# Products of the unit matrix in TensorE's planned gaps, and a new record of moves

## The chip, the cores and the metric

The kernel runs on one core of one Trainium2 chip. The metric is the device time of one execution in microseconds (us); the time before is the median of three runs. A core has a matrix engine (TensorE, PE in the profile; its weight loads are listed apart as PEld), a vector engine (DVE), a scalar engine for functions (ACT), a general engine (GpSimd, POOL), and SyncE (SP), which issues transfers here. Each engine works through its own instructions in order, and semaphores hold an instruction back until what it needs is there.

## The reference, cut to what matters

The input is four images of 128 channels and 64 x 64 pixels (4096 tokens of 128 values each). Layer 0 is a hybrid of convolution and state-space scans, layer 1 attention with a mixture of experts. What the changed code computes is layer 0, above all this scan, one for the "seed" branch and two in a cascade for each image:

```python
z = zxbcdt[..., :di]
dt = softplus(zxbcdt[..., -nh:] + dt_bias)
xBC = silu(causal_conv3(xBC) + conv_b)          # three taps along the tokens
y = ssd(xs * dt[..., None], dt * A, Bm, Cm)     # chunks of 64 tokens, a state carried from chunk to chunk
y = y + D[None, None, :, None] * xs
y = y.reshape(b, l, di) * silu(z)
y = y * rsqrt(mean(y * y, -1) + 1e-05) * rms_w  # the mean over each token's di values
return y @ out_w.T
```

After both cascades of an image come a layer norm over channels, the addition of the seed branch, and a feed-forward part: two 1x1 convolutions with a depthwise 3x3 convolution and a GELU between them. Layer 1 follows (layer norm, four-headed attention over 4096 tokens, then eight experts with the best two chosen); no line of it is in the change.

## The kernel before, in words

Layer 0 works in blocks of 512 tokens, eight to an image, always with all 128 channels on the partitions. A block's passage through one scan is an item. Items of the seed branch come first (8 of them, for all four images at once), then the two cascades of each image, the second two blocks behind the first: 8 + 64 = 72 items. Each item passes through four stages, `outer` (loading, norm), `prep` (time steps, decays), `front` (the five products, transposes, states) and `back` (products within chunks, gate, norm, output). In one step of the loop, item s is in `front`, s - 1 in `back`, s + 1 in `prep`, s + 2 in `outer`, and the feed-forward part of the image before may run along. So one step holds one `back`; below it is called a stage of the program, and its length is that from one `ps_ms` to the next.

In `back`, lines 622 to 721, TensorE forms the products `bank` (named `py` in the code) within chunks, DVE adds their halves to `y` (`scalar_tensor_tensor` in `within`), POOL multiplies by the gate (`zs`, `nc.gpsimd.tensor_mul`), ACT squares the result into `y`, and TensorE takes the mean of the squares with the product `ps_ms`. ACT forms the reciprocal root of it, and TensorE's product `ps_out` gives the item's output. The products `ps_yo`, `ps_d`, `ps_z`, `ps_x`, `ps_B`, `ps_C`, `pt_b`, `pt_x`, `ps_g` and `ps_st` belong to `front` and to the next `back`.

The instructions are not issued as the stages call them. The class `Deck` (line 773) records every operation of layer 0 with what it depends on and with a price; a run of TensorE calls into one tile counts as one operation, `Op` (line 757). `Deck.flush` (line 911) then plays the five engines through in a small model: each takes, of its operations that are ready, the one of the highest rank, if its tiles have room in their ring of buffers. The rank is the order of recording, less an entry of the table `BEHIND` (line 878) for stage, engine and, where one is given, tile: a positive entry lets an operation wait behind later ones, a negative one draws it forward. These entries, found by a search over the model, are what the change calls the record of moves. The resulting order, `order`, is what is issued, all from one line, the call of `getattr` in `flush` (line 1040): so all of layer 0 stands under L1040 in the profile, and has to be told apart by tiles.

For TensorE the model keeps a list `worked` of busy stretches. An operation is priced at twice its cost where the last `COLD[0]` = 4.0 us held more than `COLD[1]` = 2.0 us of idle time:

```python
busy_for = sum(b - max(a, start - span) for a, b in worked)
slow = 2 if span - busy_for > most else 1
```

There are two flushes: one for the whole of layer 0 but the last image's feed-forward part, and one for that part, which runs together with the first projections of layer 1. Most short-lived products in PSUM (`ps_ms`, `ps_out`, `ps_cd`, `pt_x`, `ps_mean` and others) share one ring of two tiles, `psw`.

Of the kernel before, what the change touches and what calls it, by code (L numbers as in the profile page):

```python
# [46 lines left out]
class Spec:  # L47


    def __init__(self, nh, n, nl, row0, rows):  # L50
        self.nh, self.n, self.nl = nh, n, nl
        self.row0, self.rows = row0, rows
        self.ng = nl // 4
        self.np = nl // 2
        self.di = nh * 8

        self.iB, self.iC, self.ix, self.iz, self.idt = 0, 384, 768, 1344, 1536
        self.nw = 1536 + 128 * self.np
# [697 lines left out]

class Op:
    __slots__ = ("engine", "calls", "cost", "deps", "users", "waits", "ready", "rank", "uses", "set",
                 "phase", "stage", "mode", "out", "src", "both")

    def __init__(self, engine):
        self.engine, self.calls, self.cost, self.deps, self.users = engine, [], 0.0, set(), []
        self.ready, self.rank, self.uses, self.set, self.phase = 0.0, 0.0, {}, None, None
        self.out = self.src = self.mode = None
        self.both = False


SILU, GELU, EXPS = "silu", "gelu", "exps"
# [4 lines left out]
class Deck:  # L773


    def __init__(self, nc):
        self.nc, self.ops, self.seen, self.rings, self.ring_of = nc, [], {}, {}, {}
        self.phase, self.stage, self.held = None, None, set()
        self.make, self.made, self.both, self.count = {}, {}, {}, 0
        for name in ("vector", "scalar", "gpsimd", "tensor", "sync"):  # L780
            setattr(self, name, Recorder(self, name))

# [58 lines left out]
    def price(self, engine, name, args, kw, out, ins, op):  # L841
# [36 lines left out]
        ("back", "gpsimd"): 70, ("back", "gpsimd", "last0_casc1"): 120, ("back", "scalar"): -50,  # L878
        ("back", "scalar", "A_casc1"): -200, ("back", "scalar", "e"): -40, ("back", "sync"): 40,
        ("back", "sync", "gfd"): -10, ("back", "sync", "hl"): 120, ("back", "sync", "raw"): -40,  # L880
        ("back", "sync", "td"): 110, ("back", "tensor", "ps_d"): -70, ("back", "tensor", "ps_out"): 120,
        ("back", "tensor", "py"): 120, ("back", "vector", "A_casc1"): -200, ("back", "vector", "bdt_casc1"): 140,
        ("back", "vector", "biasB_casc1"): 40, ("back", "vector", "biasC_casc1"): 200, ("back", "vector", "raw"): 10,
        ("back", "vector", "wc_casc1"): -120, ("ffn", "gpsimd", "h1_1"): 70, ("ffn", "scalar"): 10,
        ("ffn", "sync", "gf8"): 30, ("ffn", "tensor", "ps_gmix"): 10, ("ffn", "tensor", "ps_mean"): 40,
        ("ffn", "tensor", "ps_var"): 10, ("ffn", "vector", "acc"): 140, ("ffn", "vector", "t"): -40,
        ("front", "gpsimd", "last_casc1"): -10, ("front", "scalar"): 20, ("front", "scalar", "Bc"): -20,
        ("front", "scalar", "Cc"): -400, ("front", "scalar", "bT"): -40, ("front", "scalar", "cd"): 240,
        ("front", "scalar", "rt"): -10, ("front", "scalar", "zs"): -70, ("front", "tensor"): 20,
        ("front", "tensor", "ps_ea"): -120, ("front", "tensor", "ps_g"): -120, ("front", "tensor", "ps_st"): 180,  # L890
        ("front", "tensor", "ps_x"): 20, ("front", "tensor", "ps_z"): -10, ("front", "tensor", "pt_x"): 40,
        ("front", "vector", "gm"): 20, ("front", "vector", "ps_st"): -20, ("front", "vector", "xd"): -200,
        ("front", "vector", "xp0"): -10, ("front", "vector", "xp3"): 30, ("front", "vector", "y"): -200,
        ("outer", "gpsimd"): -200, ("outer", "gpsimd", "halo_seed"): 200, ("outer", "gpsimd", "last0_casc0"): 120,
        ("outer", "scalar"): 40, ("outer", "scalar", "hi"): -120, ("outer", "scalar", "ln_r"): -20,
        ("outer", "scalar", "xin"): 200, ("outer", "sync", "raw"): 20, ("outer", "sync", "wc_seed"): -10,
        ("outer", "sync", "xin"): -40, ("outer", "tensor"): 110, ("outer", "tensor", "ps_tok"): 40,
        ("outer", "vector"): -20, ("outer", "vector", "A_seed"): 200, ("outer", "vector", "W_casc0"): 200,
        ("outer", "vector", "bdt_casc0"): 10, ("outer", "vector", "bdt_seed"): 10,
        ("outer", "vector", "biasB_casc0"): 20, ("outer", "vector", "biasB_seed"): -10,  # L900
        ("outer", "vector", "biasx_seed"): 200, ("outer", "vector", "raw"): 70, ("outer", "vector", "wc_casc0"): 10,
        ("prep", "gpsimd"): 190, ("prep", "gpsimd", "cdx"): 10, ("prep", "gpsimd", "halo_seed"): 10,
        ("prep", "gpsimd", "x4"): -40, ("prep", "scalar", "ah"): -40, ("prep", "scalar", "cde"): -70,
        ("prep", "sync", "x4"): 90, ("prep", "tensor", "ps_cd"): 10, ("prep", "vector", "acs"): -190,
        ("prep", "vector", "sdT"): -70,
    }
    LAG = 0.05
    COLD = 4.0, 2.0
# [2 lines left out]
    def flush(self, tc):  # L911
# [4 lines left out]
        opening = set()  # L916
# [11 lines left out]
        for i, op in enumerate(ops):  # L928
            op.rank = -i - self.BEHIND.get((op.stage, op.engine), 0) - self.BEHIND.get(
                (op.stage, op.engine, op.out.rsplit("_", 1)[0]), 0)  # L930
        room, head = dict(self.rings), {}
        phases, whole = {}, {}
        for op in ops:
            if op.set == SILU:
# [9 lines left out]
        now, table, lock, mode, worked = 0.0, None, None, None, deque()  # L944
        lockers = {"vector": 0.0, "gpsimd": 0.0}
        while events:
            now = events[0][0]
            while events and events[0][0] <= now + 1e-9:
                _, kind, i = heappop(events)
                op = ops[i]  # L950
                if kind == 0:
                    heappush(ready[op.engine], (-op.rank, i))
                elif kind == 1:
                    for t in op.uses:
                        left[t] -= 1
                        if left[t] == 0:
                            room[self.ring_of[t]] += 1
                    for j in op.users:
                        ops[j].waits -= 1
                        if ops[j].waits == 0:  # L960
                            lag = 0.02 if ops[j].engine == op.engine and op.engine != "sync" else self.LAG
                            heappush(events, (now + lag, 0, j))
            for e in engines:
# [3 lines left out]
                while ready[e]:  # L967
                    key = heappop(ready[e])
                    op = ops[key[1]]
# [27 lines left out]
                    continue  # L997
                i = chosen[1]
                op = ops[i]
                for t in [t for t in op.uses if t not in opening]:  # L1000
                    opening.add(t)
                    room[self.ring_of[t]] -= 1
                    head[self.ring_of[t]] = head.get(self.ring_of[t], 0) + 1
                start = now
                if e == "tensor" and op.mode != mode:
                    mode = op.mode
                    start += 0.1
                if e == "tensor":

                    span, most = self.COLD  # L1010
                    while worked and worked[0][1] < start - span:
                        worked.popleft()
                    busy_for = sum(b - max(a, start - span) for a, b in worked)
                    slow = 2 if span - busy_for > most else 1
# [19 lines left out]
        for i in order:  # L1034
            op = ops[i]
            if op.set == EXPS and table != EXPS:
                self.nc.scalar.preload_act_table_set(LNEXP)
            table = op.set or table
            for name, args, kw in op.calls:
                getattr(getattr(self.nc, op.engine), name)(  # L1040
                    *[self.real(a) for a in args], **{k: self.real(a) for k, a in kw.items()})
# [112 lines left out]
def layer0(tc, T, td, const, ident, eps, where, batches, qkv):  # L1154
# [9 lines left out]
    with ExitStack() as ctx:  # L1164
# [10 lines left out]
        both, first = const, where["const"]["ms_seed"][0]  # L1175
# [34 lines left out]
        nc.vector.tensor_add(bias2, P("n2b"), P("detok_b"))  # L1210

        deck = Deck(nc)
        nc = sh.nc = deck

        def ring(stack, name, bufs, **kw):
            return deck.ring(stack.enter_context(tc.tile_pool(name=name, bufs=bufs, **kw)), bufs, kw.get("space"))
# [303 lines left out]
        last = ring(ctx, "last", 2)  # L1520
# [525 lines left out]
```

## Time and profile before

| | |
|---|---|
| median of three runs | 8313.97 us (8304.8 to 8316.73) |
| the profiled execution | 8310.76 us, its span 8309.0 us |
| start and group norm, 0 to 200 us | TensorE busy 107.19 us, clock 0.81 |
| 200 to 476.5 us, mostly the seed items | TensorE busy 226.94 of 276.5 us, clock 0.85 |
| cascades without feed-forward, 476.5 to 1328.7 us | TensorE busy 729.94 of 852.2 us, clock 0.91 |
| cascades with feed-forward, 1328.7 to 3431.2 us | TensorE busy 1846.73 of 2102.5 us, clock 0.93 |
| the last image's feed-forward, 3500 to 3675 us | TensorE busy 153.59 of 175 us, clock 0.93 |
| layer 1, 3675 to 8309 us | TensorE busy 4489.99 of 4634 us, clock 0.99 |

The page of the profile gives an engine's busy time and its share of the span, then the span in 40 slices with a busy digit per engine (9 is 90% or more) and, as PEclk, the clock that TensorE was granted, in tenths of full speed. Rows of stretches name a start and an end, and for each engine the busy time and the number of instructions in it, the mean clock, the share of the transfer engines and GB/s. Rows in order of time give start, duration, engine, line, operation, the tile written and those read, and in square brackets the idle time of the engine before it with what ended it. A row of waits names the engine and tile that waited, what it waited for, the total in us, the number of waits, and the longest. In the profile a float32 product counts as two products with two weight loads, a transpose as one.

### The profile page before, as it was taken

What the parts mean: (1) busy time and instruction counts of PE and PEld (TensorE: products, weight loads), DVE (VectorE), ACT (ScalarE), POOL (GpSimd) and SP (SyncE); (2) the same over time, 40 slices, a digit from 0 to 9 for tenths busy, and PEclk for the clock granted to TensorE, in tenths of its full rate; (3) what the DMA queues carried; (4) which work ended last, traced back from release to release, by engine and by line L of the source; (5) the groups of instructions that cost most, each with busy time, mean ns of one, the idle gap of its engine ahead of it and who ended that gap; (6) DMA issues with size and microseconds to landing.
All of it is one profiled execution on the core that took longest, in us unless ns stands there. A gap on an engine that the chain in (4) does not pass through costs nothing.

```text
span 8309.0 us, 191474 instructions
## 1 busy us (share of the span) xinstructions
PE 7600.4 (91%) x80284; PEld 4516.6 (54%) x80284; DVE 6299.9 (76%) x11211; ACT 5103.8 (61%) x6517; POOL 4892.5 (59%) x3441
## 2 busy tenths in 40 slices
PE   5888888888888898779999999999999999999998
PEld 3566666666666666434555555555555545555554
DVE  5676768887888788776777777777777777777775
ACT  5767767777777777545555555555555555555554
POOL 1111111211122112119999999999999999999997
PEclk7889999999999899889999999999999999999999
DMA  4221112221112121145544445444545454444442
GB/s 139 83 56 48 43 53 57 54 57 54 52 55 59 54 62 46 54 133 139 129 126 124 127 123 130 127 126 126 129 121 136 122 135 122 120 116 121 116 121 59
DMA packets 306606, 800.55 MB, mean 96 GB/s; under 512 B 43985, under 2 KB 61009, under 8 KB 288849
## 3 DMA queue, kind: packets, MB, share of 16 engines
q1 hardware_dynamic: 304848, 780.94, 35.8%
q8 instruction: 633, 10.37, 0.5%
q10 hardware_dynamic: 432, 5.12, 0.2%
q14 instruction: 229, 1.87, 0.1%
q0 software_dynamic: 464, 2.25, 0.1%
HBM read 595.19 MB, written 192.94 MB: 95 GB/s over the span
## 4 chain that ended last, share of the span: by engine, by line
PE 29%; POOL 22%; issue 3%; DVE 2%; ACT 1%; DMA 1%; SPq 0%; POOLq 0%; DVEq 0%
POOL s L1894 13%; PE ps_mx L1850 7%; PE acc L1909 6%; POOL es L1896 6%; PE ps_s L1888 6%; PE ps_s L1882 3%; PE ps_e L1798 2%; PE ps_den L1922 1%; DVE mx L1852 1%; PE ps_taps L1040 1%; PE ps_sh L1869 0%; POOL parts L1712 0%; POOL cx L1714 0%; PE ps_f L1787 0%; PE ps_f L1786 0%
## 5 line engine op out<-in xcount | busy, mean ns | idle before, releaser
L1852 DVE TENSOR_REDUCE mx<-ps_mx 128x1 f32<-128x512 f32 x4096 | 2789.8, 689 | 815.0 <-PE ps_mx L1850 807.8
L1892 ACT ACTIVATE e<-ps_s 128x1024 f32<-128x1024 f32 x2048 | 1985.3, 1022 | 1715.6 <-PE ps_s L1888 1610.8
L1894 POOL TENSOR_TENSOR s<-e 128x1024 f32<-128x1024 f32 x1024 | 2442.2, 2385 | 206.7 <-ACT e L1892 203.5
L1850 PE MATMUL ps_mx<-k,q 128*128 128x512 f32 x4096 | 1876.1, 467 | 63.5 <-DVE mx L1852 25.3
L1896 POOL TENSOR_TENSOR es<-s 128x512 f32<-128x512 f32 x1024 | 1311.7, 1281 | 80.3
L1888 PE MATMUL ps_s<-q,k 128*128 128x512 f32 x4096 | 1279.5, 394 | 0.0
L1909 PE MATMUL acc<-e,V 128*32 128x512 f32 x8192 | 1095.2, 607 | 0.0
L1850 PEld LDWEIGHTS ps_mx<-k,q 128*128 128x128 f32 x4096 | 772.7, 189 | 532.1 <-DVE mx L1852 221.9
L1040 POOL TENSOR_TENSOR zs<-y,zs 128x256 f32<-128x256 f32 (+1 forms) x288 | 302.7, 1052 | 1153.0 <-DVE y L1040 1152.2
L1888 PEld LDWEIGHTS ps_s<-q,k 128*128 128x128 f32 x4096 | 772.6, 189 | 137.8 <-issue 2.9
L1040 DVE SCALAR_TENSOR_TENSOR e<-e,gm 128x1024 f32<-128x1024 f32 (+1 forms) x576 | 668.0, 1175 | 54.8 <-ACT e L1040 53.3
L1882 PEld LDWEIGHTS ps_s<-mr,ones 32*128 32x128 f32 x4096 | 201.4, 182 | 890.5 <-ACT e L1892 411.1
L1040 ACT ACTIVATE e<-ps_d 128x1024 f32<-128x1024 f32 (+1 forms) x576 | 546.5, 975 | 86.1 <-PE ps_d L1040 63.4
L1882 PE MATMUL ps_s<-mr,ones 32*128 32x512 f32 x4096 | 531.9, 496 | 20.3 <-ACT e L1892 20.3
L1040 DVE SCALAR_TENSOR_TENSOR y<-bank,const,y 128x128 f32<-128x128 f32 (+1 forms) x1152 | 364.2, 338 | 234.4 <-PE bank L1040 233.7
L1040 PE MATMUL bank<-e,xp 64*32 64x128 f32 x17408 | 459.0, 283 | 63.6 <-DVE y L1040 51.1
L1040 PEld LDWEIGHTS bank<-e,xp 64*32 64x32 f32 x17408 | 369.4, 110 | 134.9 <-DVE y L1040 73.7
L1040 PE MATMUL ps_d<-rt,lt 32*128 32x256 f32 x4352 | 406.7, 312 | 32.3 <-ACT e L1040 10.8
L1040 PEld LDWEIGHTS ps_d<-rt,lt 32*128 32x128 f32 x4352 | 294.6, 190 | 194.0 <-issue 50.1
L1909 PEld LDWEIGHTS acc<-e,V 128*32 128x32 f32 x8192 | 161.7, 108 | 362.6 <-issue 356.5
L1805 DVE SCALAR_TENSOR_TENSOR acc<-ps_e,w,acc 128x128 f32<-128x128 f32 x896 | 312.5, 349 | 47.7 <-PE ps_e L1798 15.0
L1040 DVE SCALAR_TENSOR_TENSOR acc<-h,pb,acc 128x512 f32<-128x512 f32 x448 | 330.4, 757 | 7.5
(349 smaller groups left out, 11503.7 us busy)
## 6 DMA issues: line engine op xcount, KB each, us to landing
k<-kd SPq DMA_DIRECT2D x512, 512.0 KB
x<-hl SPq DMA_DIRECT2D x256, 256.0 KB
V<-vd SPq DMA_DIRECT2D x128, 512.0 KB
cd<-raw SPq DMA_DIRECT2D x256, 256.0 KB
parts<-cd SPq DMA_DIRECT2D x128, 512.0 KB
xin<-in_x SPq DMA_DIRECT2D x128, 256.0 KB
q<-qd SPq DMA_DIRECT2D x512, 64.0 KB
hl<-hi SPq DMA_DIRECT2D x72, 256.0 KB
```

The source lines that it names most:

```text
L1040: getattr(getattr(self.nc, op.engine), name)(*[self.real(a) for a in args], **{k: self.real(a) for k, a in kw.items()})
L1798: nc.tensor.matmul(pe, lhsT=xl[:, tok], rhs=ew[:, e:e + 2, :].rearrange("p e c -> p (e c)"), start=True, stop=True)
L1805: nc.vector.scalar_tensor_tensor(acc, pe[:, 128 * j:128 * j + 128], we, acc, ALU.mult, ALU.add)
L1850: nc.tensor.matmul(p, lhsT=q4s[u][:, 128 * qt:128 * qt + 128], rhs=k4s[u][:, blk(kb)], start=True, stop=True)
L1852: nc.vector.tensor_reduce(mxs[u][:, qt, kb:kb + 1], p, AX.X, ALU.max)
L1882: nc.tensor.matmul(pts[j // 2][:, j % 2, :], lhsT=ones2[rows, :], rhs=mrows[u][rows, :], start=True, stop=False)
L1888: nc.tensor.matmul(pts[j // 2][:, j % 2, :], lhsT=k4s[u][:, 128 * kt:128 * kt + 128], rhs=q4s[u], start=False, stop=True)
L1892: nc.scalar.activation(e[:, 2 * j:2 * j + 2], pts[j], AF.Exp)
L1894: nc.gpsimd.tensor_add(s2, e[:, 0:2], e[:, 2:4])
L1896: nc.gpsimd.tensor_add(s, s2[:, 0], s2[:, 1])
L1909: nc.tensor.matmul(accs[u][32 * j:32 * j + 32, :], lhsT=Vs[u][:, 4 * g + j, :], rhs=e[:, j, :], start=g == 0, stop=g == 7)
L1922: nc.tensor.matmul(p[32 * j:32 * j + 32, :], lhsT=ones, rhs=s, start=True, stop=True)
```

## The change

Where the model sees TensorE idle before an operation that opens its output tile, the plan now puts plain products of the 128 x 128 unit matrix `ident` with itself into that tile, 128 columns wide. The operation then overwrites the tile as before (its first product has `start=True`), so nothing of what is computed changes. Their number is 60% of the gap at a price of 0.22 us, for gaps over 1 us; the gap is counted from the end of TensorE's last work or from the time when a buffer of the ring came free (`freed`), whichever is later. The model also counts them as work when it looks for slow stretches. Second, many entries of `BEHIND` are new. The same fills come into both flushes.

```diff
 class Op:
     __slots__ = ("engine", "calls", "cost", "deps", "users", "waits", "ready", "rank", "uses", "set",
-                 "phase", "stage", "mode", "out", "src", "both")
+                 "phase", "stage", "mode", "out", "src", "both", "fill")
...
-        ("back", "sync", "td"): 110, ("back", "tensor", "ps_d"): -70, ("back", "tensor", "ps_out"): 120,
-        ("back", "tensor", "py"): 120, ("back", "vector", "A_casc1"): -200, ("back", "vector", "bdt_casc1"): 140,
+        ("back", "sync", "td"): 110, ("back", "tensor", "ps_d"): -70, ("back", "tensor", "ps_out"): -70,
+        ("back", "tensor", "py"): 120, ("back", "vector", "A_casc1"): -400, ("back", "vector", "bdt_casc1"): 140,
...
+        ("back", "vector", "wc_casc1"): -120, ("back", "vector", "ys"): -130, ("ffn", "gpsimd", "h1_1"): 70,
+        ("ffn", "scalar"): 30, ("ffn", "scalar", "h1_0"): -10, ("ffn", "sync", "gf8"): 30,
+        ("ffn", "tensor", "ps_det"): -40, ("ffn", "tensor", "ps_gmix"): 10, ("ffn", "tensor", "ps_hh"): -40,
+        ("ffn", "tensor", "ps_mean"): 40, ("ffn", "tensor", "ps_var"): 20, ("ffn", "vector", "acc"): 130,
...
-        ("outer", "scalar"): 40, ("outer", "scalar", "hi"): -120, ("outer", "scalar", "ln_r"): -20,
+        ("outer", "tensor", "ps_tok"): -280, ("outer", "vector"): -20, ("outer", "vector", "A_seed"): 200,
...
-        ("prep", "gpsimd"): 190, ("prep", "gpsimd", "cdx"): 10, ("prep", "gpsimd", "halo_seed"): 10,
-        ("prep", "gpsimd", "x4"): -40, ("prep", "scalar", "ah"): -40, ("prep", "scalar", "cde"): -70,
-        ("prep", "sync", "x4"): 90, ("prep", "tensor", "ps_cd"): 10, ("prep", "vector", "acs"): -190,
-        ("prep", "vector", "sdT"): -70,
+        ("prep", "scalar", "ah"): 240, ("prep", "scalar", "cde"): -70, ("prep", "sync", "x4"): 100,
+        ("prep", "tensor", "ps_cd"): 10, ("prep", "vector", "a2"): 200, ("prep", "vector", "acs"): -190,
+        ("prep", "vector", "sdT"): -110,
...
                         if left[t] == 0:
                             room[self.ring_of[t]] += 1
+                            freed[self.ring_of[t]] = now
...
-                for t in [t for t in op.uses if t not in opening]:
+                opens_now = [t for t in op.uses if t not in opening]
+                for t in opens_now:
...
                     span, most = self.COLD
+                    op.fill = 0
+                    if self.ident is not None and op.out in opens_now:
+                        last = worked[-1][1] if worked else 0.0
+                        gap = now - max(last, freed.get(self.ring_of[op.out], 0.0))
+                        op.fill = int(0.6 * gap / 0.22) if gap > 1.0 else 0
+                        worked.append((now - 0.22 * op.fill, now))
...
+            if op.fill:
+                self.real(op.calls[0][2].get("out", op.calls[0][1][0] if op.calls[0][1] else None))
+                at = self.made[op.out]
+                at = at[:, 0, 0:128] if len(at.shape) == 3 else at[:, 0:128]
+                for _ in range(op.fill):
+                    self.nc.tensor.matmul(at, lhsT=self.ident, rhs=self.ident, start=True, stop=True)
...
         deck = Deck(nc)
+        deck.ident = ident
```

More of the change, by code (lines that the diff above doesn't have):

```diff
@@ L764, in __init__ @@
         self.out = self.src = self.mode = None
-        self.both = False
+        self.both, self.fill = False, 0
 SILU, GELU, EXPS = "silu", "gelu", "exps"
@@ L779, in __init__ @@
         self.make, self.made, self.both, self.count = {}, {}, {}, 0
+        self.ident = None
         for name in ("vector", "scalar", "gpsimd", "tensor", "sync"):
@@ L880 @@
         ("back", "sync", "gfd"): -10, ("back", "sync", "hl"): 120, ("back", "sync", "raw"): -40,
-        ("back", "sync", "td"): 110, ("back", "tensor", "ps_d"): -70, ("back", "tensor", "ps_out"): 120,
-        ("back", "tensor", "py"): 120, ("back", "vector", "A_casc1"): -200, ("back", "vector", "bdt_casc1"): 140,
-        ("back", "vector", "biasB_casc1"): 40, ("back", "vector", "biasC_casc1"): 200, ("back", "vector", "raw"): 10,
-        ("back", "vector", "wc_casc1"): -120, ("ffn", "gpsimd", "h1_1"): 70, ("ffn", "scalar"): 10,
@@ L885 @@
[L885 to L894, printed above, removed]
@@ L895 @@
-        ("outer", "scalar"): 40, ("outer", "scalar", "hi"): -120, ("outer", "scalar", "ln_r"): -20,
[L896 to L899, printed above, removed]
@@ L900 @@
-        ("outer", "vector", "biasB_casc0"): 20, ("outer", "vector", "biasB_seed"): -10,
-        ("outer", "vector", "biasx_seed"): 200, ("outer", "vector", "raw"): 70, ("outer", "vector", "wc_casc0"): 10,
-        ("prep", "gpsimd"): 190, ("prep", "gpsimd", "cdx"): 10, ("prep", "gpsimd", "halo_seed"): 10,
-        ("prep", "gpsimd", "x4"): -40, ("prep", "scalar", "ah"): -40, ("prep", "scalar", "cde"): -70,
-        ("prep", "sync", "x4"): 90, ("prep", "tensor", "ps_cd"): 10, ("prep", "vector", "acs"): -190,
@@ L905 @@
-        ("prep", "vector", "sdT"): -70,
+        ("back", "sync", "td"): 110, ("back", "tensor", "ps_d"): -70, ("back", "tensor", "ps_out"): -70,
+        ("back", "tensor", "py"): 120, ("back", "vector", "A_casc1"): -400, ("back", "vector", "bdt_casc1"): 140,
+        ("back", "vector", "biasB_casc1"): 40, ("back", "vector", "biasC_casc1"): 400, ("back", "vector", "raw"): 20,
+        ("back", "vector", "wc_casc1"): -120, ("back", "vector", "ys"): -130, ("ffn", "gpsimd", "h1_1"): 70,
+        ("ffn", "scalar"): 30, ("ffn", "scalar", "h1_0"): -10, ("ffn", "sync", "gf8"): 30,
@@ new lines @@
+        ("ffn", "tensor", "ps_det"): -40, ("ffn", "tensor", "ps_gmix"): 10, ("ffn", "tensor", "ps_hh"): -40,
+        ("ffn", "tensor", "ps_mean"): 40, ("ffn", "tensor", "ps_var"): 20, ("ffn", "vector", "acc"): 130,
+        ("ffn", "vector", "gmix"): -20, ("ffn", "vector", "t"): -40, ("front", "gpsimd"): 20,
+        ("front", "gpsimd", "last_casc1"): -10, ("front", "scalar", "Bc"): 20, ("front", "scalar", "Cc"): -400,
+        ("front", "scalar", "bT"): -40, ("front", "scalar", "cd"): 260, ("front", "scalar", "rt"): -10,
@@ new lines @@
+        ("front", "scalar", "zs"): -70, ("front", "tensor"): 20, ("front", "tensor", "ps_ea"): -120,
+        ("front", "tensor", "ps_g"): -120, ("front", "tensor", "ps_st"): 180, ("front", "tensor", "ps_x"): 20,
+        ("front", "tensor", "ps_z"): -10, ("front", "tensor", "pt_x"): 40, ("front", "vector", "gm"): 20,
+        ("front", "vector", "ps_st"): -20, ("front", "vector", "xd"): -200, ("front", "vector", "xp0"): -20,
+        ("front", "vector", "xp3"): 30, ("front", "vector", "y"): -200, ("outer", "gpsimd", "halo_casc0"): -40,
@@ new lines @@
+        ("outer", "gpsimd", "halo_seed"): 200, ("outer", "gpsimd", "last0_casc0"): 120, ("outer", "scalar"): 40,
+        ("outer", "scalar", "ln_r"): -20, ("outer", "scalar", "xin"): 200, ("outer", "sync", "raw"): 20,
+        ("outer", "sync", "wc_seed"): -10, ("outer", "sync", "xin"): -40, ("outer", "tensor"): 110,
+        ("outer", "tensor", "ps_tok"): -280, ("outer", "vector"): -20, ("outer", "vector", "A_seed"): 200,
+        ("outer", "vector", "W_casc0"): 200, ("outer", "vector", "bdt_casc0"): 10,
@@ new lines @@
+        ("outer", "vector", "bdt_seed"): 10, ("outer", "vector", "biasB_casc0"): 20,
+        ("outer", "vector", "biasB_seed"): -10, ("outer", "vector", "biasC_seed"): -10,
+        ("outer", "vector", "biasx_seed"): 400, ("outer", "vector", "wc_casc0"): 10, ("prep", "gpsimd"): 190,
+        ("prep", "gpsimd", "cdx"): 10, ("prep", "gpsimd", "halo_seed"): 10, ("prep", "gpsimd", "x4"): -40,
+        ("prep", "scalar", "ah"): 240, ("prep", "scalar", "cde"): -70, ("prep", "sync", "x4"): 100,
+        ("prep", "tensor", "ps_cd"): 10, ("prep", "vector", "a2"): 200, ("prep", "vector", "acs"): -190,
@@ L930, in flush @@
                 (op.stage, op.engine, op.out.rsplit("_", 1)[0]), 0)
-        room, head = dict(self.rings), {}
+        room, head, freed = dict(self.rings), {}, {}
         phases, whole = {}, {}
```

## The prediction

> **What bounds the kernel now.** I read first the page's busy shares and its 40 slices, to see where the changed code runs and what TensorE's clock does there:
>
> ```profile
> PE 7600.4 (91%) x80284; PEld 4516.6 (54%) x80284; DVE 6299.9 (76%) x11211; ACT 5103.8 (61%) x6517; POOL 4892.5 (59%) x3441
> ...
> PE   5888888888888898779999999999999999999998
> ...
> PEclk7889999999999899889999999999999999999999
> ```
>
> A slice is 8309.0/40 = 208 us. The changed code makes layer 0, slices 1 to 17. From slice 18 on, layer 1 isn't touched: its 4634 us stay, and so does all but a few us of the first 200. Next I asked for busy time and clock by stretches; columns are PE, PEld, DVE, ACT and POOL busy, clock, DMA share, GB/s:
>
> ```profile
> 200.00:3470.00 3270.00, 2831.20 (x52906) 2029.28 (x52904) 2537.55 (x4304) 2416.76 (x3245) 581.99 (x718) 0.92 0.19 54
> 714.80:763.40 48.60, 42.02 (x794) 30.75 (x794) 30.78 (x52) 33.75 (x43) 6.67 (x9) 0.89 0.04 13
> 902.00:947.70 45.70, 39.10 (x794) 28.50 (x794) 30.79 (x52) 33.62 (x43) 6.69 (x9) 0.95 0.04 14
> ```
>
> The main part of layer 0 has TensorE busy 2831 of 3270 us, 87%, more than any other engine (DVE 78%). The last two rows are two stages of the same kind: the same 794 products and 52, 43 and 9 operations of the other engines, with the same busy times there. TensorE alone differs: 42.02 against 39.10 us, +2.92, at clock 0.89 against 0.95; the stage is 48.60 against 45.70 long, +2.90. So time that TensorE loses to its clock is paid in full.
>
> How does the clock fall? Rows of the same view, cut where it changes:
>
> ```profile
> 2004.78:2008.19 3.41, 1.98 (x128) 1.87 (x128) 3.41 (x9) 0.61 (x3) 0.48 (x1) 1.00 0.02 5
> 2008.19:2011.61 3.42, 1.46 (x6) 0.50 (x6) 3.42 (x7) 1.85 (x4) 1.70 (x3) 1.00 0.00 0
> 2011.61:2015.02 3.41, 3.09 (x49) 1.40 (x52) 3.41 (x7) 1.49 (x3) 1.72 (x1) 0.50 0.41 154
> 2015.02:2018.43 3.41, 3.31 (x116) 2.85 (x108) 2.12 (x5) 1.79 (x3) 0.34 (x1) 1.00 0.84 259
> ```
>
> The clock is 1.00 or 0.50 and changes only on a grid of 3.41 us. A window in which TensorE worked 1.46 of 3.42 us is followed by one at half clock; that one, busy 3.09 us, by full clock again. Counting all windows from 200 to 3450 us in this way: of 118 at full clock with TensorE busy about 2.0 us or less, 79 were followed by half clock; of 682 that were busier, 3. A window therefore tolerates about 1.4 us of idle time. Between 200 and 3470 us 84 stretches at half clock begin, 522 us together (the mean clock says the same: (1 - 0.92) x 2 x 3270 = 523), and TensorE is busy in 456 of them. At full clock that work takes half: at most 228 us to win.
>
> Who makes the idle time? The waits of TensorE in 200 to 3470, then the order of time at one of them:
>
> ```profile
> PE ps_ms L1040 <- ACT y L1040: 137.4, 57, 8.8
> PE bank L1040 <- DVE y L1040: 50.8, 57, 1.4
> PE ps_st L1040 <- DVE gm L1040: 22.8, 18, 2.5
> ```
>
> ```profile
> 2004.69 2.07 PE L1040 MATMUL ps_st<-xd,bT 64*64 64x32 f32 x128 [1.11 <-DVE gm L1040]
> ...
> 2008.71 0.72 POOL L1040 TENSOR_TENSOR zs<-y,zs 128x256 f32<-128x256 f32 x1
> ...
> 2009.47 0.63 ACT L1040 ACTIVATE y<-zs 128x512 f32<-128x512 f32 x1
> 2010.15 1.08 PE L1040 MATMUL ps_ms<-y,const 128*64 128x512 f32 x4 [3.39 <-ACT y L1040]
> ```
>
> Once a stage, ps_ms waits for the square of zs, behind POOL and DVE: a fixed latency in which TensorE, in order, has nothing. Such a gap ends in the window just shown.
>
> [...]
>
> **The change part by part.** First, the fills. The changed program has 504 added products of the 128x128 unit matrix in 71 places; in its order of instructions they stand directly ahead of the first product of ps_ms nearly everywhere (4 each in 25 places, 11 each in 12). Each is two loads and two products of 128 columns. The nearest row is layer 1's product with the same matrix:
>
> ```profile
> L1787 PE MATMUL ps_f<-ident,acc x256: 274/326/378, 4003.6 to 8305.4; 128*128 128x128 f32 x128
> ```
>
> Two of these in a row take 0.49 us, so they start 0.49 - 0.326 = 0.16 us apart: 0.33 us for a fill, alone. In a row they may be denser: two 512-column products of ps_var took 1.02 us at 0.59 us each, 0.43 apart, so 128 columns 0.11 apart and a fill 0.215 us. Bounds 0.215 and 0.33 us at full clock; I take 0.215, since fills follow each other. A fill needs only the freed PSUM slot, so no new wait arises; behind it in TensorE's order stands ps_ms, which waits anyway. All fills are 108 us, hidden by those gaps so long as they are as long as planned; uncovered, they would be 108 us on the path.
>
> I set the fills ahead of each ps_ms beside the gap that the trace of before has there (69 stages from 200 us on):
>
> - A: 15 gaps over 2.5 us with 7 or more fills. Gaps 56.5 us, 172 fills = 37.0 us, leaving 1.3 us each. Half clock after them: TensorE busy 81.4 us.
> - B: 15 gaps over 2.5 us with 4 fills. Gaps 50.2, fills 12.9, leaving 2.5 each. Busy at half clock 75.0.
> - C: 15 gaps of 1.3 to 2.5 us. Gaps 28.5, 71 fills = 15.3, leaving 0.9 each. Busy 58.3.
> - D: 12 gaps under 1.3 us with 77 fills = 16.6 us in 9.9 us of gap. Busy 46.2.
> - 12 stages get none.
>
> Other idle time is (3270 - 2831 - 137)/3270 = 9%, 0.3 us of a window, so about 1.1 us may be left of a gap. C's 0.9 is below it, A's 1.3 just above and spoils a window only where it lies whole in it (2.1 of 3.41 of the phases); B's 2.5 can't be split into two parts under 1.1, only shorten what follows. I choose as averted shares 0.6 for A, 0.15 for B, 0.65 for C, 0.25 for D. Half of the busy time is won: 24.4 + 5.6 + 18.9 + 5.8 = 54.7 us. The fills longer than their gaps cost 8.1 us in D and 1.6 in C. Sum: -45 us. The 61 fills ahead of ps_tok, ps_dt and ps_ea at the start stand in waits (ps_tok 5.8 us on ACT, ps_dt 13.2 us on a DMA) and the last 39 after the last stage, among waits for transfers: I take 0 for both, bounds -6 and +3.
>
> Second, the record. New BEHIND entries move operations. In the stages that I compared, TensorE's order is the same but for single operations (ps_dt, ps_hh, ps_mean, pt_sd); ScalarE swaps lt, u and ah just ahead of the square y, DVE moves acc, ys, a and sd, some a third of its rows; 59 SyncE rows move past others, in transfers that use 0.19 of the DMA engines here. Nothing in the trace prices it: an operation in the chain to y moved by one place is about 0.7 us a stage (sd and u are 0.71 and 0.72), 50 us over 72 stages, with either sign; I take 0, with bounds of 25 us, since the moves ahead of y differ among stage kinds.
>
> The profiled execution took 8310.76 us (span 8309.0 plus 1.8 around it); 8310.76 - 45 = 8266, and the median of the three runs is 3 us above it: 8269 us.
>
> **Rivals.** More: at 0.33 us a fill, A's gaps close (0.95), B's leave 2.0 (0.45), C 0.9: 38.7 + 16.9 + 26.2 + 7 = 89, less overruns of about 22: -67, 8247 us. For it: gaps repeat exactly at 3.39 and 3.7 us; against it: D.
>
> Nothing: the moves lengthen the chain to y by 0.6 us a stage, 43 us, and take the gain: 8310 us. For it: DVE is 100% busy in the window before the wait; against it: TensorE's order hardly moved.
>
> Slower: the fills themselves become the path. TensorE is in order; a fill that stands where the real gap is short holds up ps_ms, ps_out and the next stage's ps_d. D is this already. If the changed order brings y earlier than planned in most stages, 80 us of the 108 lie on the path and some 55 are won: 8339 us. It decides when over half of the fills overrun their gaps.
>
> **How the numbers follow.** The likeliest, 0.55: 8269, own range 8250 to 8292. More, 0.15. Nothing within 0.2% (17 us, about what a measurement of this kernel can tell from no change), 0.15. Slower, 0.15. Hence faster 0.70, same 0.15, slower 0.15. The range 8215 to 8328 takes in "more" with a kind bound of the moves, and most of "nothing".
>
> **What would show it.** In 200 to about 3430 us: clock 0.95 instead of 0.92; TensorE's wait of ps_ms for y shrinks by about 75 us, with fills in its place; half-clock stretches fall from 84 to about 55; fills start at 0.22 to 0.33 us; stage lengths of the 714.8 kind become those of 902.0. I am wrong if the clock rises and the stages don't shorten (then another engine bounds), if fills stand where y was already there, or if layer 1 changes.

## The result, and the profile after

The changed kernel takes 8240.58 us, the median of four runs (8232.76 to 8252.73); before, the four runs shown with it have a median of 8309.38 (8302.88 to 8316.73). The ratio is 0.9924, with a 95% interval of 0.9906 to 0.9941: faster by 0.76%, about 63 us by the ratio and 69 us by the medians. Forecast were 45 us.

The busy shares and slices of the page after the change:

```profile
PE 7645.5 (93%) x81292; PEld 4619.0 (56%) x81292; DVE 6294.1 (76%) x11211; ACT 5112.4 (62%) x6520; POOL 4866.6 (59%) x3441
...
PE   6888889899899898889999999999999999999998
...
PEclk8999999999999999989999999999999999999999
```

TensorE has 1008 more instructions, which are the 504 fills at two products each, and is 45 us longer busy in a span 64 us shorter. The eights in the clock row of layer 0 are nines, but for the first slice and the one at layer 0's end. The same stretch as before, the two stages of one kind that correspond to those shown before, and layer 1 (columns as before):

```profile
200.00:3470.00 3270.00, 2896.91 (x53738) 2125.25 (x53735) 2563.72 (x4342) 2454.53 (x3292) 557.72 (x719) 0.95 0.20 56
684.60:730.80 46.20, 40.09 (x802) 30.26 (x802) 30.64 (x52) 33.78 (x43) 6.64 (x9) 0.96 0.04 14
868.10:914.00 45.90, 40.15 (x800) 30.42 (x800) 30.55 (x52) 33.86 (x43) 6.64 (x9) 0.95 0.04 14
3610.00:8245.00 4635.00, 4496.42 (x25536) 2345.12 (x25536) 3493.63 (x6400) 2453.77 (x2896) 4260.57 (x2641) 0.99 0.48 123
```

The clock is 0.95. Both stages last 46 us, where one lasted 48.60 before. Layer 1, with the same number of products as from 3675 to 8309 us before, takes 4635 us against 4634: everything was won in layer 0. The wait that makes the gap, and one gap in order of time:

```profile
PE ps_ms L1058 <- ACT y L1058: 76.1, 54, 4.8
PE bank L1058 <- DVE y L1058: 45.5, 50, 2.4
```

```profile
1140.56 1.14 PE L1058 MATMUL ps_st<-xd,bT 64*64 64x32 f32 x64
1141.62 2.72 PE L1056 MATMUL ps_ms<-ident 128*128 128x128 f32 x22
1145.39 1.08 PE L1058 MATMUL ps_ms<-y,const 128*64 128x512 f32 x4 [1.05 <-ACT y L1058]
...
1147.32 1.08 PE L1058 MATMUL ps_out<-zs,wc_casc 128*64 128x512 f32 x4 [0.38 <-ACT y L1058]
```

Eleven fills (22 products) take 2.72 us of a gap of 3.70, ps_ms still waits 1.05 us for y, and ps_ms and ps_out behind it run at full clock (1.00 from 1141.62 to 1148.40 us).

Counting as in the prediction, half-clock stretches that begin between 200 and 3475 us and TensorE's busy time in them, for every kernel run:

| kernel | median us | ratio to before, 95% | stretches | at half clock, us | TensorE busy in it, us |
|---|---|---|---|---|---|
| before | 8304.90 to 8313.97 | | 84 | 522 | 456 |
| the change | 8240.58 | 0.9924 (0.9906, 0.9941) | 61 | 345 | 315 |
| e1_no_fills | 8325.27 | 1.0014 (1.0008, 1.0021) | 99 | 618 | 534 |
| e2_old_order | 8263.24 | 0.9940 (0.9927, 0.9953) | 61 | 338 | 298 |
| e3_whole_gap | 8257.16 | 0.9939 (0.9926, 0.9951) | 58 | 300 | 278 |
| e4_small_fills | 8279.33 | 0.9966 (0.9953, 0.9980) | 74 | 440 | 400 |
| e5_no_seed_fills | 8253.28 | 0.9936 (0.9922, 0.9949) | 62 | 334 | 306 |
| e6_long_gaps | 8237.35 | 0.9918 (0.9905, 0.9932) | 54 | 297 | 269 |
| e7_by_profile | 8238.23 | 0.9920 (0.9906, 0.9933) | 52 | 297 | 276 |
| e8_old_record | 8261.53 | 0.9953 (0.9939, 0.9966) | 60 | 331 | 302 |
| e9_spare | 8220.87 | 0.9898 (0.9883, 0.9913) | 45 | 188 | 176 |
| e10_old_but_tok | 8256.62 | 0.9944 (0.9930, 0.9957) | 55 | 317 | 288 |
| e11_new_but_tok | 8250.69 | 0.9929 (0.9915, 0.9942) | 55 | 307 | 280 |

The runs came in three groups, each with its own runs of the kernel before (medians 8313.17 for e1 to e4, 8304.90 for e5 to e8, 8308.91 for e9 to e11), so ratios are what is compared across groups. The last three columns come from one profiled execution of each kernel, which need not lie at the median: that of e1 (8344.64 us) was the slowest of its 22, that of e2 (8248.88 us) the fastest of its five.

### The profile page after: what moved, and what is told of

Its sections match the earlier page's. It is cut to its first block, busy times and chain, and to the rows that moved or that the text cites. A ratio compares the mean times of both kernels' runs of the same rounds, so it can differ in the third digit from the quotient of the medians.

```text
span 8245.0 us, 193517 instructions
## 1 busy us (share of the span) xinstructions
PE 7645.5 (93%) x81292; PEld 4619.0 (56%) x81292; DVE 6294.1 (76%) x11211; ACT 5112.4 (62%) x6520; POOL 4866.6 (59%) x3441
## 3 DMA queue, kind: packets, MB, share of 16 engines
q0 software_dynamic: 464, 2.25, 0.1%
## 4 chain that ended last, share of the span: by engine, by line
PE 31%; POOL 21%; issue 3%; DVE 2%; ACT 1%; DMA 0%; SPq 0%; POOLq 0%; DVEq 0%; ACTq 0%
POOL s L1913 12%; PE ps_mx L1869 8%; PE acc L1928 7%; PE ps_s L1907 6%; POOL es L1915 6%; PE ps_s L1901 3%; PE ps_e L1817 2%; PE ps_den L1941 2%; DVE mx L1871 1%; PE ps_taps L1058 1%; PE ps_sh L1888 0%; POOL parts L1731 0%; PE ps_f L1806 0%; POOL cx L1733 0%; PE ps_f L1805 0%
## 5 line engine op out<-in xcount | busy, mean ns | idle before, releaser
L1058 POOL TENSOR_TENSOR zs<-y,zs 128x256 f32<-128x256 f32 (+1 forms) x288 | 297.7, 1035 | 1059.2 <-DVE y L1058 1058.7
```

The source lines that it names most:

```text
L1058: getattr(getattr(self.nc, op.engine), name)(*[self.real(a) for a in args], **{k: self.real(a) for k, a in kw.items()})
```

## The experiments

**Fills or moves: the change's order without its fills.** The plan is that of the change to the last instruction; the fills are left out when the order is issued.

```diff
-            if op.fill:
+            if False:
```

> The changed kernel's order of instructions exactly, the 504 fills not issued. My theory (the fills keep the clock up, the moves of the record are worth nothing): 8300 to 8320 us, as before the change; clock from 200 to 3400 us back at 0.92, about 84 stretches at half clock. Rival (the moves are the gain, the fills little): 8240 to 8260 us. If both have a part, the time lies between, and its distance from before is the part of the moves.

Measured: 8325.27 us, ratio 1.0014. The moves alone gain nothing; they lose 12 us (7 to 17), and the time is 5 us above the first theory's range. The wait of ps_ms in this kernel, and its stretch:

```profile
PE ps_ms L1058 <- ACT y L1058: 160.2, 62, 3.9
```

```profile
200.00:3470.00 3270.00, 2846.92 (x52618) 2036.39 (x52616) 2512.86 (x4253) 2416.09 (x3231) 543.68 (x709) 0.91 0.19 54
```

The gaps are longer than before the change (160.2 against 137.4 us), the half-clock stretches more (99 against 84), the clock lower. From here to the change, in one and the same order, the fills bring 1.0014 - 0.9924 = 0.9%, 75 us.

**Fills alone: the old order with fills.** Here the record is that of before, and the fills aren't counted as work in the plan, so the order of all other instructions is exactly the old one. Against the change:

```diff
-                        worked.append((now - 0.22 * op.fill, now))
...
 (and BEHIND as before)
```

> The order of the kernel before exactly, with 460 fills put into the gaps that its own plan has. My theory: 45 to 60 us less than before, 8250 to 8265 us, half-clock stretches between 200 and 3470 us from 84 to about 60. Rival (the moves are the gain): 8295 us or more.

Measured: 8263.24 us, ratio 0.9940, 50 us less than before (39 to 61), with 61 stretches. The first theory holds: the fills work by themselves, and by nearly what the tally said. Together the two runs show that the parts don't add: the moves cost 12 us without fills (0.14%), and with fills the change is 0.0016 below this kernel, 13 us. That last difference is smaller than the two intervals together, and e8 below gives a second reading of it. The wait of ps_ms with the fills in the old order, and the stretch:

```profile
PE ps_ms L1055 <- ACT y L1055: 57.4, 47, 3.2
```

```profile
200.00:3470.00 3270.00, 2884.09 (x53725) 2106.35 (x53722) 2561.72 (x4356) 2444.96 (x3288) 592.92 (x723) 0.95 0.20 56
```

**More fills everywhere.** The number of fills in each place is multiplied by five thirds and rounded down, 808 in all.

```diff
-                for _ in range(op.fill):
+                for _ in range(op.fill * 5 // 3):
```

> The changed kernel's order, with five thirds as many fills, so that the whole planned gap is filled. My theory: the gaps that had 4 fills keep 1.8 us open instead of 2.3, those with 11 close; half-clock stretches from 61 to about 45, 15 to 25 us less than the change: 8215 to 8225 us. Rival (fills come onto the path): where the real gap is shorter than planned, 30 us of fills are late, and the time is 8260 us or more.

Measured: 8257.16 us, ratio 0.9939. The first theory falls: half clock shrinks to 300 us, but the time doesn't; it lies 3 us below the rival's number. The rival's mechanism is there. In one item with feed-forward work beside it, in order of time:

```profile
1439.00 2.72 PE L1056 MATMUL ps_ms<-ident 128*128 128x128 f32 x22
1441.65 1.08 PE L1058 MATMUL ps_ms<-y,const 128*64 128x512 f32 x4
1442.66 1.12 PE L1058 MATMUL ps_det<-gf,pb 8*128 8x512 f32 x2
```

ps_ms no longer waits for anything; in the trace, y was ready 1.60 us before it began. Summed over the items from 200 us on, fills run for 31 us after y was ready, against 6.8 us in the change. TensorE's work at half clock is 37 us less than in the change, worth by estimate at most 18 us (half of it, at clock 0.50); late fills are 24 us more. That the one eats the other is this sum, and no run shows it apart.

**Is it the clock, or something else that the fills do?** The same number of fills, their products as long in time, in a smaller part of the array (64*32 in the trace instead of 128*128). "The gate" in what was expected stands for whatever it is that puts TensorE's clock at 1.00 or 0.50.

```diff
-                    self.nc.tensor.matmul(at, lhsT=self.ident, rhs=self.ident, start=True, stop=True)
+                    self.nc.tensor.matmul(at[0:32], lhsT=self.ident[0:64, 0:32], rhs=self.ident[0:64], start=True, stop=True)
```

> As the change, each fill with only 64 rows and 32 columns of the unit matrix loaded, still 128 columns streamed: as long in time, an eighth of the array. If the gate counts the time in which TensorE works (what I assumed in setting fills beside busy time): as the change, 8235 to 8250 us. Rival (it counts how much of the array works): most of the gain of the fills is lost, 8280 us or more, with about as many half-clock stretches as without fills.

Measured: 8279.33 us, ratio 0.9966, between the two theories' numbers. The fills ahead of ps_ms, products and weight loads (shortest, median and longest in ns, first and last start), in the change:

```profile
L1056 PE MATMUL ps_ms<-ident x784: 269/275/580, 128.0 to 3402.6; 128*128 128x128 f32 x196
L1056 PEld LDWEIGHTS ps_ms<-ident x784: 186/192/338, 128.0 to 3402.5; 128*128 128x128 f32 x196
```

and in this kernel:

```profile
L1056 PE MATMUL ps_ms<-ident x784: 266/269/418, 128.5 to 3433.6; 64*32 64x128 f32 x196
L1056 PEld LDWEIGHTS ps_ms<-ident x784: 102/107/174, 128.5 to 3433.5; 64*32 64x32 f32 x196
```

The products last nearly as long (269 ns in the median against 275, and eleven of them 2.59 us against 2.72), stand in the same places, leave as much of the wait of ps_ms (78.3 us against 76.1), and are late by about as little (8.1 us). Yet half clock is 440 us instead of 345, and the time half-way back to e1's. TensorE's products fill the same time, there is less clock, and less gain: it is the clock that the fills work through. What in TensorE's work the clock follows is less clear. An eighth of the array did about half of what whole fills do: the mean clock of all executions is 0.950 in e1, 0.960 here and 0.969 in the change, and of the 85 us between the medians of e1 and the change 46 are won here. (The single traces of the table would give 65%, but that of e1 is its slowest execution.) So the time of the products alone (269 ns against 275) doesn't set the clock. But the weight loads too are shorter here, 107 ns against 192, so whether the part of the array or the loading counts is not told apart.

**Which fills are late, and which gaps are still open?** In the change's trace two things stand out by item: in the first five items y is long ready when ps_ms begins, and in 15 later ones 2.2 to 3.4 us of the gap stay open. Here is one of the first, at half clock (0.50 from 159.99 to 162.06 us), four fills in 2.07 us directly ahead of ps_ms:

```profile
159.99 2.07 PE L1056 MATMUL ps_ms<-ident 128*128 128x128 f32 x8
161.85 1.27 PE L1058 MATMUL ps_ms<-y,const 128*128 128x512 f32 x2
```

Three kernels count the items as they are issued and set the number of fills, in the change's order: the first, the second, and both with fewer fills in seven late items. In the lines below LONG stands for the twelve items of the second, and the notes at the right say which kernels have the line.

```diff
+            if op.out.startswith("ps_ms") and op.engine == "tensor":
+                item += 1
+                op.fill = 0 if item < 5 else op.fill                                   # e5, e7
+                op.fill = 10 if item in LONG else 9 if item in (34, 50, 66) else op.fill   # e6, e7
+                op.fill = {37: 4, 46: 4, 53: 4, 62: 4, 61: 0, 69: 3, 70: 9}.get(item, op.fill)   # e7
```

> The change without the 20 fills ahead of ps_ms in the first five items, where the trace of the change shows the square of zs ended 1.45 to 3.2 us before ps_ms begins. If those fills lie on the path: 20 fills of 0.22 to 0.49 us, 4 to 9 us less than the change, 8232 to 8237 us. Rival (TensorE's work there leads nowhere before the next wait, or the fills keep the clock up): no difference from the change, within 5 us, or slower.

> The change with more fills only where its trace shows long steady gaps: 10 in place of 4 in the twelve items whose gap is about 3.4 us with 2.3 left, 9 in place of none in three items with 3.2 us (119 fills more). If the left-over of 2.3 us is what still spoils windows there: some 12 half-clock stretches and 60 us of half clock less, 20 to 28 us less than the change, 8213 to 8221 us. Rival (half clock then comes from the other gaps just after, as those at ps_ea and ps_d): under 8 us less.

> Both of the runs above together, and fewer fills in seven items where ps_ms begins after y was ready (61 fewer than the sum): the sum of their gains and 2 to 4 us, 8205 to 8215 us. Rival (a stage shortened in one place waits in the next): no better than the better of the two.

(By the instructions in the traces the second has 99 fills more than the change, not 119, and the third 21 fewer than the sum, not 61.)

Measured: 0.9936, 0.9918 and 0.9920, all within the change's interval. Without the late fills nothing is won: the ratio is even 0.0012 higher, which is within the noise. With the long gaps filled, stretches that follow mostly on a gap at ps_ms fall from 16 to 5, as was meant; half clock falls only by 48 us, and the gain is 5 us or nothing, where 20 to 28 were expected. The rival of e6 is what the trace shows: 14 of its 54 stretches, 102 us, follow mostly on gaps at ps_ea, as 13 with 89 us did in the change. Both together are no better than the second.

**The record, with fills.** The change with the table of before, its plan counting fills as work.

> The change with the record of before: the plan counts its fills as work, and 443 are issued. With the old order and fills put in afterwards the time was 8263, with the new record 8241. If the new record brings the 22 us: 8255 to 8270. Rival (counting the fills as work in the plan brings it, whatever the record): 8235 to 8248.

Measured: 8261.53 us, ratio 0.9953 (443 fills). As in e2, the old record is the slower one once there are fills, by 13 us there and 24 us here. Each difference alone is at the edge of the noise: the change's interval ends at 0.9941, those of e2 and e8 begin at 0.9927 and 0.9939. So the sign is likely, the size uncertain; how the plan counts them makes no difference that can be told. In the profiles the difference lies in the first eight items (counted from 0, as in the code): they take 285.8 and 297.7 us in the two kernels with the old record and fills, 275.7 in the change; from item 8 to item 70 it is 2964 and 2962 against 2965 us. Single executions differ here too: e6, which has the change's instructions in these eight items, takes 279.7. Without fills the first eight items gain as well (279.9 us in e1, 292.0 before), and what the new record costs lies behind them (3044 us against 3006 from item 8 to item 70), though part of that is e1's slow profiled execution. Of the record's entries the one that draws the seed items' first product forward is that for ps_tok, so it was set alone in both directions.

```diff
-        ("outer", "tensor"): 110, ("outer", "tensor", "ps_tok"): 40, ("outer", "vector"): -20,
+        ("outer", "tensor"): 110, ("outer", "tensor", "ps_tok"): -280, ("outer", "vector"): -20,
```

> e8_old_record (fills, record of before; ratio to before 0.995) with one entry of the new record: ps_tok of the stage outer at -280 instead of 40, which draws the seed items' first product forward. If the new record's 22 us come from the seed items and through this entry: ratio about 0.993, and the first eight items 12 to 20 us shorter in the profile. Rival (many small moves in all items): ratio 0.9945 to 0.996.

> The change with that one entry set back to 40. If the entry carries the record's gain: ratio to before about 0.9945 to 0.9955. Rival: as the change, 0.9915 to 0.993.

Measured: 0.9944 with this entry in the old record, 0.9929 with it taken out of the new one; the first eight items take 288.0 and 281.5 us. Neither number can be told from its neighbour without the switch (0.9953 and 0.9924). So ps_tok is not shown to bring the record's part, no other entry was tried alone, and which of them do stays open.

**The gaps that a fill can't reach.** At ps_ea and ps_yo the operation's own tile isn't free while TensorE is idle, so from 200 us on the change puts nothing there. This kernel adds to e6 29 groups of fills (165 fills) into a spare tile of the ring psw, wherever the plan has TensorE idle for over 1 us and both tiles of that ring free; the order stays.

```diff
+                    idle = now - (worked[-1][1] if worked else 0.0)
...
+                    w = (id(self.psw), "w")
+                    if self.psw is not None and not op.fill and idle > 1.0 and room.get(w) == 2:
+                        op.spare = int(0.6 * min(idle, 4.0) / 0.22)
...
+            if op.spare:
+                at = self.psw.tile([128, LB], F32, tag="w", name="fill")[:, 0:128]
+                for _ in range(op.spare):
+                    self.nc.tensor.matmul(at, lhsT=self.ident, rhs=self.ident, start=True, stop=True)
```

> e6_long_gaps with 29 more groups of fills, in gaps that the plan has ahead of operations whose own tile isn't free yet (ps_ea, ps_yo, ps_z, ps_d): they go into a spare tile of the other ring, where the plan has both of its tiles free. In e6_long_gaps 14 of the 54 half-clock stretches, 102 us, follow mostly on gaps at ps_ea. If those can be averted in this way: 8 to 10 fewer stretches, 8215 to 8228 us (ratio to before about 0.990). Rival (where the real gap is shorter than planned the fills are late, and ps_ea's are ahead of the path): 8237 us or more, ratio 0.992 or above.

Measured: 8220.87 us, ratio 0.9898 (0.9883 to 0.9913), the fastest of all, some 20 us below the change. Against e6 alone it is 0.0020, 17 us, about as much as the two intervals together can tell. Its stretch of layer 0:

```profile
200.00:3470.00 3270.00, 2931.01 (x54299) 2157.55 (x54299) 2589.16 (x4382) 2470.42 (x3321) 562.74 (x721) 0.97 0.20 58
```

The clock is 0.97, half clock 188 us, and the stretches that follow on ps_ea fall from 14 (102 us) to 6 (24 us). Of the 45 that remain, 13 follow mostly on gaps at bank, where TensorE waits for DVE's y, which reads bank (45.8 us in 52 waits from 200 to 3400 us).

## Why the prediction was right, and where it was off

**Where the time is, and the mechanism**: right. e2 and e1 show the fills' gain in both orders, e4 that it goes through the clock. The thirteen profiled executions say the same: plotted against half of TensorE's busy time at half clock (the last column of the table), their spans lie within 17 us of one straight line, over 128 us from the fastest to the slowest. Clock 0.95 was forecast and measured; stretches fell from 84 to 61 (55 forecast), the wait of ps_ms for y by 61 us (75 forecast); layer 1 didn't move. The time itself, 8240.58 us, is 9 us below the range of 8250 to 8292 that the likeliest course was given; by the ratio, 0.9924 of 8313.97, it is 8251 and at that range's edge.

**The fills' price**, 0.215 us chosen between 0.215 and 0.33: from four to eleven fills the time goes from 1.16 to 2.72 us, 0.223 us a fill. At half clock four take 2.07 us, 1.8 times as long. **Late fills**, 9.7 us: 6.8 us from 200 us on, so the sum was about right, but not its places. Some 4 us of it are items 3 and 4, which were in class D; the five items that were to bring most of D's 8.1 us (39, 40, 44, 55, 56) have no late fill at all, because in the change's order the gaps there are longer than in the trace of before, and the fills end before y is ready. e5 shows no gain from leaving out the late fills of the first items.

**The tally of the fills, -45 us**: on the old order, whose gaps it used, e2 measures -50 (39 to 61), with 460 fills in place of the 504 of the tally. That the two agree is in part luck, for two of its terms were off in opposite directions. The averted shares gave 54.7 us of TensorE's time; in e2 the busy time at half clock fell from 456 to 298 us; half of the difference, taken as won as in the prediction, is 79. And the step "time that TensorE loses to its clock is paid in full", read from one pair of stages without feed-forward work, is too high on the average: the straight line through the thirteen executions falls by about 0.7 us for each us of TensorE's time so saved. It isn't a fixed share. From profiled execution to profiled execution, 62 of 79 us reached the end from before to e2 (78%), 98 of 110 from e1 to the change, but 30 of 70 from the change to e9. What the rest is spent on wasn't traced; other engines' waits are the likely answer, not a shown one.

**The record, taken as 0**: this is the mis-sized term. Alone it costs 12 us; with fills it brings 13 us by e2 and 24 by e8, both at the edge of the noise. It lies within the bounds of 25 us that were set, but it isn't one number: its value depends on the fills, and a sum of parts can't hold that. If these readings hold, it is the larger part of what lies between 45 and the 63 to 69 us measured.

**The rivals.** "More", at 8247 us, came closest in time, for another reason than the one given: fills weren't dearer, and the long gaps stayed as open as the tally had them. "Nothing" didn't happen. "Slower", late fills, is a real mechanism: e3 has 31 us of them, about what its higher clock should have brought, but at 60% of the planned gap they are few.

## What to carry to other kernels

Where an engine's clock follows its recent work, as TensorE's did here, a gap costs twice: its own length (3.39 us ahead of the ps_ms at 2010.15 us, before the change), and the slow window behind it (3.41 us at clock 0.50 there). Cheap work that needs only a free tile can fill such a gap, if it is sized from the gap with room left over (60% of it here, ratio 0.9924); filling the whole planned gap cut half clock from 345 to 300 us and won no time (ratio 0.9939). And when one kind of gap is filled, look at which gap stands ahead of the slow windows next: e9 won some 17 us there, filling the first kind better (e6) won 5 or nothing.

## What wasn't expected of the hardware

Fills in an eighth of the array, with products nearly as long (269 ns against 275) but shorter weight loads (107 ns against 192), still brought about half of what whole ones bring, in clock (0.960, between 0.950 without fills and 0.969 with whole ones) and in time (46 of 85 us).

The edge at which a window of 3.41 us costs the next one its clock is narrower than the prediction's count shows. Before the change, of the windows at full clock from 200 to 3450 us, all 57 with TensorE busy under 1.75 us were followed by half clock, 23 of the 62 between 1.75 and 2.25 us, and 3 of the 682 above (the prediction counts the first two kinds together). After the change it was 29 of the 32 below, 25 of the 77 in the middle and 7 of the 742 above.
